# A table-lookup convolution block on one Trainium2 core: the distance matmuls of a step split around the lookup products, and the accumulator given a bank of its own

## The chip, the cores and the metric

The kernel runs on one core of one Trainium2 chip. The time is the device time of one execution in microseconds (us). Before the change it was 2782.4 us, the median of three runs that lie between 2776.88 and 2785.29.

## What is computed

The input x has 16 images of 256 channels and 28x28 pixels. It is normalized over groups of 8 channels (32 groups) and passed through two "convolutions by lookup"; then come a squeeze-and-excite gate and two residual additions. One such convolution, cut to what matters:

```
def amm_conv3x3(x, centroids, w_sub):            # centroids: C x 16 x 9
    p = patches of 3x3, one 9-vector per channel and pixel
    d = |p|^2 - 2 p.centroids + |centroids|^2    # 16 distances per channel, pixel
    attn = softmax(-d)
    lut = einsum('cks,cso->cko', centroids, w_sub)
    return einsum('bnck,cko->bno', attn, lut)
out = relu(bn(amm_conv3x3(gn(x), c1, w1)))
out = bn(amm_conv3x3(out, c2, w2))
out = relu(se(out) + gn(x));  result = x + out
```

The kernel does not build lut. It multiplies the softmax with the centroids again (this gives 9 soft-quantized values per channel and pixel) and then multiplies these by w_sub.

## The kernel before

**Blocks and steps.** An image in a layer is four blocks: two halves of the pixels (392 each, 14 rows) by two halves of the channels (128 each). That is 4 x 16 images x 2 layers = 128 blocks. A block j has two steps, 2j and 2j+1, so there are 256 steps and seven more that only finish the last image. Everything is entered in one table by `at(step, place, function, ...)`; the table is sorted, and each engine issues its instructions in that order, engine by engine, with nothing reordered behind it (`manual_schedule`). So a fractional place such as 0.1 or 2.0 is the order inside one step.

**What TensorE does in a step, in this order.**

- *logits* (places 0.1 and 0.2, line 350 and on, matmul in line 356): two rounds. A round has 16 tiles of 32x32 (4 groups of rows by 4 of columns), each of 392 columns, in 4 PSUM banks. All matmuls are in fp32 and appear as two passes in the profile, so a round is 32 matmul instructions and 32 weight loads, and a step 64 and 64.
- *num_b* (place 1.3, even steps only, line 417): sums of the exponentials, 64 instructions on 64x32 tiles, 2 banks.
- *num_a* (line 403): exponentials by centroids, 64x32 tiles; two calls (32 instructions, 4 banks) in each step.
- *product* (place 2.0, line 485): the lookup product, 9 (or in two steps of each image 3 and 6) full 128x128 matmuls, that is 18 (6, 12) passes, into one bank. An image needs seven such products, because a 2x2 block product is formed with seven multiplications; `mix` (GpSimd, lines 492 and 494) forms the differences of the blocks, and `combine` (line 188) those of the weights S1 to S4 in the first layer.

**The other engines.** ScalarE takes the exponentials out of PSUM (`exps`, line 368, entered right behind each logits round at 0.12 and 0.22), splits num_b's result (lines 428, 430) and copies half of num_a's (line 471). VectorE takes the reciprocal (line 443), spreads it over the rows (lines 454, 458) and scales the other half of num_a's (line 477). GpSimd scales and mixes (lines 466, 492, 494). VectorE or ScalarE take the product out of its bank at place 0.0 of the next step (`acc_add` line 522, `acc_copy` line 516). In the second layer, the first round of half of the blocks is not exponentiated at once: it is copied (`wide_copy`, line 374), its maximum is taken on VectorE, subtracted on GpSimd (line 388) and only then does ScalarE take the exponential (line 396).

**PSUM.** All eight banks form one ring, `bank(name)`; each allocation takes the next bank and waits until what was there eight allocations ago has been read. An even step takes 4 + 4 + 2 + 4 + 1 banks and an odd one 4 + 4 + 4 + 1.

**Loads.** The patches of a step are fetched from DRAM by six transfers (`patches`, lines 342 and 346) from SyncE's queue, issued at place 0.5 two steps ahead, because there are two patch buffers; in the first five steps half of them are issued by GpSimd. SyncE's queue also carries the normalized images (line 335), inputs, stores (line 814) and the preparation of the second layer's tables.

**The end.** For the last image the normalized input is made at place 0.9 of its step 13 (`finish_norm`, line 789), into a buffer that has one copy (`tag="pb"`); flags for the rare unsafe case are made at place 0.95 of its step 11 (`flags`, line 825), into the same buffer. The squeeze-and-excite matmuls (lines 757 and 770) use weights padded to 128 columns.

The lines that set the order of a step's TensorE work:

```
for q in range(2):
    mm = 2 * p + q
    at(g + p, 0.1 + 0.1 * q, logits, u, mm)
    ...
        at(g + p, 0.12 + 0.1 * q, exps, u, mm)
at(g + 2, 1.3, num_b, u)
...
    at(g + 2, 1.35, num_a, u, mm)
...
    at(g + c - (c == 5 and n == 0), 2.0, product, (n, c), us[r], w, ks)
```

Of the kernel before, what the change touches and what calls it, by code (L numbers as in the profile page):

```python
# [23 lines left out]
N = RT * W  # L24
# [12 lines left out]
NPT = 2  # L37
# [30 lines left out]
def kernel(  # L68
# [20 lines left out]
    nc = tc.nc  # L89
    B, C, _ = x.shape  # L90
    NB = C // P
    RED = se_w1.shape[1]

    const = ctx.enter_context(tc.tile_pool(name="const", bufs=1))
    dram = ctx.enter_context(tc.tile_pool(name="dram", bufs=1, space=DRAM))
    small = ctx.enter_context(tc.tile_pool(name="small", bufs=2))
    p_ring = ctx.enter_context(tc.tile_pool(name="p_ring", bufs=8, space=PSUM))

    gmat = const.tile([P, P], F32, name="gmat")
    make_block_diagonal(nc, gmat, 8)  # L100
    ctx.enter_context(tc.manual_schedule())

    def bank(name):
        return p_ring.tile([P, 512], F32, tag="ps", name=name)

    def view(t, off, dims):
# [76 lines left out]
    def combine(n):  # L183
        a, b, op = {
            "S1": ("S3", "A22", ALU.add), "S2": ("S1", "A11", ALU.subtract),
            "S4": ("A12", "S2", ALU.subtract), "S3": ("A11", "S3", ALU.subtract),
        }[n]
        nc.vector.tensor_tensor(wl[n], wl[a], wl[b], op)

    nhalf_sb = load(nhalf, "nhalf_sb")  # L190
    load_wd(None, 0)
# [3 lines left out]
    load_wd(None, 1)  # L195
    load_cw(0, 1)
    vecs = load(vec, "vecs", nc.gpsimd)
    w1_sb = [nhalf_sb, const.tile([P, P], F32, name="w1_sb")]
    w2_sb = const.tile([P, C], F32, name="w2_sb")
    b1_sb = const.tile([P, 1], F32, name="b1_sb")  # L200

    def load_se():
        for t in (*w1_sb, w2_sb, b1_sb):
            nc.gpsimd.memset(t, 0.0)
        for k in range(NB):
            nc.sync.dma_start(w1_sb[k][:, :RED], se_w1[k * P : (k + 1) * P, :])
        nc.sync.dma_start(w2_sb[:RED], se_w2)
        nc.sync.dma_start(b1_sb[:RED], se_b1.rearrange("(p o) -> p o", o=1))


    m_lo, m_hi, zero = kst[:, 0:1], kst[:, 1:2], kst[:, 2:3]
    m_cw = kst[:, 3:7]
# [537 lines left out]

    def se_hidden(b):
        ysum = ys[b, "sum"]
        ps = bank("sep")[:, :1]
        n = 0
        for k in range(NB):
            for i in range(2):
                nc.tensor.matmul(
                    ps, lhsT=w1_sb[k], rhs=ysum[:, k, i : i + 1],
                    start=(n == 0), stop=(n == 2 * NB - 1),
                )  # L760
                n += 1
        hid = small.tile([P, 1], F32, name="se_hid")
        nc.scalar.activation(hid, ps, AF.Relu, bias=b1_sb, scale=1.0 / HW)
        se[b] = hid

    def se_gate(b):
        hid = se[b]
        ps = bank("sep")[:, :NB]
        for k in range(NB):
            nc.tensor.matmul(  # L770
                ps[:, k : k + 1], lhsT=w2_sb[:, k * P : (k + 1) * P], rhs=hid, start=True, stop=True
            )
        gt = small.tile([P, NB], F32, name="se_gt")
        for k in range(NB):
            nc.scalar.activation(
                gt[:, k : k + 1], ps[:, k : k + 1], AF.Exp, bias=nb2_sb[:, k : k + 1], scale=-1.0
            )
        nc.vector.tensor_scalar_add(gt, gt, 1.0)  # L778
        nc.vector.reciprocal(gt, gt)  # L779
        se[b] = gt  # L780
# [4 lines left out]

    def finish_norm(b, k):
        if k == 0:
            ys[b, "t"] = io.tile([P, 1568], F32, tag="pb", name="xn")
        nc.scalar.activation(
            ys[b, "t"][:, HW * k : HW * k + HW], xs[b][:, k], AF.Identity,  # L790
            bias=nrm[:, b, 2, k : k + 1], scale=nrm[:, b, 1, k : k + 1],
        )
# [48 lines left out]
    def at(cl, sub, f, *a, **kw):  # L841
        jobs.setdefault((cl, sub), []).append((f, a, kw))
# [20 lines left out]
    for j, u in enumerate(blocks):  # L863
        g = 2 * j
        u["w"] = j
        wide = u["l"] == 1 and u["hh"] == 0
        for p in range(2):
            u["pt", p] = pts[p]
            at(g + p - NPT, 0.5, patches, u, p, nc.gpsimd if g + p < 5 else None)
            for q in range(2):  # L870
                mm = 2 * p + q
                at(g + p, 0.1 + 0.1 * q, logits, u, mm)
                if wide and mm == 0:
                    at(g, 0.12, wide_copy, u, mm)
# [12 lines left out]
        for mm in range(2):  # L887
            at(g + 2, 1.35, num_a, u, mm)
            at(g + 2, 1.45, copy_a, u, mm)
            at(g + 3, 1.8, spread, u, mm)  # L890
            at(g + 3, 1.8, scale_q, u, mm)
        for mm in range(2, 4):
            at(*((g + 2, 1.8) if mm == 2 else (g + 3, 0.05)), spread, u, mm)
            at(g + 3, 1.0, num_a, u, mm)
            at(g + 3, 1.1, scale_a, u, mm)

    for l in range(2):
        for b in range(B):
# [1 line left out]
            g = 8 * n  # L900
            us = blocks[4 * n : 4 * n + 4]
            for c, (w, r, ks) in PRODUCTS.items():
                at(g + c - (c == 5 and n == 0), 2.0, product, (n, c), us[r], w, ks)
            for mm in (4, 2, 3, 0, 1):
                at(g + 5, 2.5, mix, us[0], mm, us[1], us[0])
                at(g + 7, 2.5 if mm < 2 else 1.75, mix, us[1], mm, us[2], us[1])
# [36 lines left out]
            else:  # L943
# [25 lines left out]
    for hh in range(2):  # L969
        at(6, 2.7, keep_wd, hh)  # L970
    for o in range(2):
# [223 lines left out]
```

## Time and profile before

| | before |
|---|---|
| median of three runs | 2782.4 us |
| the profiled execution's own time | 2758.4 us |
| its span (first to last instruction) | 2756.9 us |
| TensorE busy | 2670.6 us (97%) |
| GpSimd / VectorE / ScalarE busy | 2073.0 / 1730.1 / 1454.2 us (75 / 63 / 53%) |
| DMA engines, mean share in the second half | about 0.5 |
| granted TensorE clock, mean | 0.988 |

The profile shows one execution, which took 2758.4 us, 0.9% less than the median of the runs. "Busy" of TensorE counts time in which some matmul is under way; up to 16 of them are, side by side, and their ends are modelled, so that 97% does not say how full the array is. PEld are TensorE's weight loads. An entry "x64" of the timeline is 64 instructions merged; the first number is the start of the first of them and the second the time to the end of the last. In brackets stands how long the engine sat idle before it and who released it.

### The profile page before, as it was taken

The numbers are of one execution on the slowest core, as the hardware profiler recorded it, in microseconds if no ns is written. First come the engines' busy times: TensorE is split into PE (matmuls) and PEld (weight loads), VectorE is DVE, ScalarE is ACT, GpSimd is POOL, SyncE is SP. The second block draws the span as 40 slices with busy tenths as digits, with TensorE's granted clock in tenths as the row PEclk, the third lists the DMA queues.
The fourth block names the chain that finished last, engine by engine and source line by source line (L and its number), as shares of the span: only waits on it lengthen the run. The fifth ranks groups of instructions, "written<-read, shape, count | busy, mean of one in ns | idle before, by whom it ended". The sixth has DMA issues, their size and how long they took to land. (4 is left out here: it accounts for less than half of the span.)

```text
span 2756.9 us, 88069 instructions
## 1 busy us (share of the span) xinstructions
PE 2670.6 (97%) x37076; PEld 1312.1 (48%) x37076; DVE 1730.1 (63%) x3945; ACT 1454.2 (53%) x3277; POOL 2073.0 (75%) x1427
## 2 busy tenths in 40 slices
PE   5699999999999999999999999999999999999997
PEld 2344444444444444444444455444444444444444
DVE  4866555565655565655576766666766666766664
ACT  3344455545455445455445566656565656555653
POOL 4656877668877767866678787788887788877787
PEclk9899999999999999999999999999999999999998
DMA  8564677546677656666575455445455545555541
GB/s 194 135 131 115 181 196 198 154 110 158 158 189 188 155 125 156 161 165 152 120 182 121 102 120 123 116 103 114 114 120 122 116 105 111 116 118 122 117 106 47
DMA packets 223281, 374.51 MB, mean 136 GB/s; under 512 B 30424, under 2 KB 193592, under 8 KB 222880
## 3 DMA queue, kind: packets, MB, share of 16 engines
q1 hardware_dynamic: 215744, 334.53, 52.6%
q0 software_dynamic: 7136, 34.27, 3.6%
q8 instruction: 296, 4.85, 0.8%
q14 instruction: 105, 0.86, 0.1%
HBM read 288.91 MB, written 79.80 MB: 134 GB/s over the span
## 5 line engine op out<-in xcount | busy, mean ns | idle before, releaser
L368 ACT ACTIVATE e<-lg 128x392 f32<-128x392 f32 x1920 | 777.7, 527 | 814.6 <-PE lg L356 812.3
L494 POOL TENSOR_TENSOR qp<-qp,qp 128x784 f32<-128x784 f32 x512 | 938.6, 1863 | 22.9 <-DVE qp L477 22.9
L485 PE MATMUL acc<-qp,w_S 128*128 128x392 f32 x2048 | 708.3, 496 | 5.2 <-POOL qp L494 5.2
L466 POOL TENSOR_TENSOR qp<-qp,rb 128x784 f32<-128x784 f32 x256 | 470.7, 1861 | 204.4 <-DVE rb L458 204.4
L356 PE MATMUL lg<-pt,wd 32*32 32x392 f32 x16384 | 535.2, 503 | 43.9 <-DVE half_sum L522 18.7
L458 DVE STREAM_SHUFFLE rb<-r 128x392 f32<-128x392 f32 x1024 | 551.2, 603 | 0.0
L485 PEld LDWEIGHTS acc<-qp,w_S 128*128 128x128 f32 x2048 | 387.4, 191 | 306.0 <-issue 15.9
L485 PE MATMUL acc<-qp,w_A 128*128 128x392 f32 x1536 | 521.2, 492 | 0.0
L437 DVE SCALAR_TENSOR_TENSOR r<-nb,kst,r 128x392 f32<-128x392 f32 x128 | 79.8, 623 | 563.4 <-ACT r L428 547.3
L403 PE MATMUL na<-e,cwa 64*32 64x392 f32 x8192 | 409.0, 496 | 3.9 <-issue 3.9
L485 PEld LDWEIGHTS acc<-qp,w_A 128*128 128x128 f32 x1536 | 291.8, 190 | 213.8
L417 PE MATMUL nb<-e,cwb 64*32 64x392 f32 x8192 | 371.2, 496 | 0.0
L356 PEld LDWEIGHTS lg<-pt,wd 32*32 32x32 f32 x16384 | 232.0, 103 | 274.8 <-issue 171.4
L443 DVE RECIPROCAL r<-r 128x392 f32<-128x392 f32 x128 | 331.8, 2592 | 0.0
L466 POOL TENSOR_TENSOR qo<-qo,rb 128x392 f32<-128x392 f32 x128 | 131.1, 1024 | 259.2 <-DVE rb L454 259.1
L477 DVE TENSOR_TENSOR qp<-na,rb 128x392 f32<-128x392 f32 x512 | 252.3, 555 | 64.6 <-PE na L403 61.7
L403 PEld LDWEIGHTS na<-e,cwa 64*32 64x32 f32 x8192 | 146.4, 106 | 230.2 <-ACT e L368 125.0
L417 PEld LDWEIGHTS nb<-e,cwb 64*32 64x32 f32 x8192 | 143.2, 107 | 220.6 <-issue 138.3
L471 ACT COPY qp<-na 128x392 f32<-128x392 f32 x512 | 211.6, 513 | 3.9 <-PE na L403 3.9
L428 ACT ACTIVATE r<-nb,kst 128x392 f32<-128x392 f32 x128 | 87.6, 685 | 102.7 <-PE nb L417 100.1
L492 POOL TENSOR_TENSOR qo<-qo,qo 128x392 f32<-128x392 f32 x128 | 130.8, 1022 | 2.2
L374 ACT COPY e<-lg 128x392 f32<-128x392 f32 x128 | 52.9, 500 | 150.6 <-PE lg L356 150.6
(146 smaller groups left out, 1810.7 us busy)
## 6 DMA issues: line engine op xcount, KB each, us to landing
pt<-home SPq DMA_DIRECT2D x768, 209.0 KB
pt<-home SPq DMA_DIRECT2D x753, 104.5 KB
home<-xpad SPq DMA_DIRECT2D x31, 899.0 KB
xt<-in_x SPq DMA_DIRECT2D x30, 784.0 KB
out_dram<-y SPq DMA_DIRECT2D x32, 392.0 KB
w_S<-d_wS SPq DMA_DIRECT2D x4, 576.0 KB
st<-in_wsub SPq DMA_DIRECT2D x4, 512.0 KB
st<-d_wa SPq DMA_DIRECT2D x16, 128.0 KB
```

The lines of the kernel that those rows point to most:

```text
L356: nc.tensor.matmul(bk[32 * c : 32 * c + 32, :N].rearrange("p (r w) -> p r w", w=W), lhsT=wts["wd", u["hh"]][32 * i : 32 * i + 32, mm, c, : ...
L368: nc.scalar.activation(eg[:, i, :], bk[:, :N], AF.Exp, scale=2.0)
L403: nc.tensor.matmul(bs[r][32 * i : 32 * i + 32, :N], lhsT=wts["cwa", u["hh"]][64 * r : 64 * r + 64, mm, i, :], rhs=es[64 * r : 64 * r + 64, ...
L417: nc.tensor.matmul(bs[r][32 * i : 32 * i + 32, :N], lhsT=wts["cwb", u["hh"]][64 * r : 64 * r + 64, mm, i, :], rhs=es[64 * r : 64 * r + 64, ...
L443: nc.vector.reciprocal(u["r"], u["r"])
L458: nc.vector.stream_shuffle(rb[:, r, :], u["r"], mask_of(2 * mm + r))
L466: nc.gpsimd.tensor_tensor(q, q, u.pop(("rb", mm)), ALU.mult)
L471: nc.scalar.copy(u["q", 2 * mm + r], bk[:, :N])
L477: nc.vector.tensor_mul(u["q", 2 * mm + r], bk[:, :N], rb[:, r, :])
L485: nc.tensor.matmul(accs[key][:, :N], lhsT=wl[w][:, k, :], rhs=us["q", k], start=first and n == 0, stop=last and n == len(ks) - 1,)
L492: nc.gpsimd.tensor_tensor(out_u["q", 8], in0["q", 8], in1["q", 8], ALU.subtract)
L494: nc.gpsimd.tensor_tensor(pair(out_u, mm), pair(in0, mm), pair(in1, mm), ALU.subtract)
```

## The change

1. *Placement.* Each product is issued in two parts (places 2.0 and 2.05, the first with half of the factors, rounded up). The first of a step's two logits rounds moves to place 2.04 of the step before, between these parts; its exponentials follow at 2.06. The second stays at 0.1. So TensorE's order in a step becomes: one logits round, num_b, num_a, first part of the product, the next step's other logits round, second part of the product.
2. *Banks.* The ring has seven banks; the eighth belongs to the product alone.
3. *Combine.* S2 and S4 are formed by GpSimd in place of VectorE; S2 is entered at 2.65 and not 1.96 of step 7.
4. *Squeeze and excite.* The two halves of the weights are stored side by side (32 columns), so that the first product has 32 output rows; the gate takes one matmul in place of two, after one more small ScalarE instruction.
5. *The end.* `finish_norm` of the last image goes to place 0.4 of step 12, `flags` to 0.65 of step 11, and both write into a free buffer of the exponentials in place of the single `pb` buffer.
6. *The start.* The very first step's six patch transfers are all issued from SyncE's queue.

```diff
-    p_ring = ctx.enter_context(tc.tile_pool(name="p_ring", bufs=8, space=PSUM))
+    p_ring = ctx.enter_context(tc.tile_pool(name="p_ring", bufs=7, space=PSUM))
+    p_acc = ctx.enter_context(tc.tile_pool(name="p_acc", bufs=1, space=PSUM))
...
     def bank(name):
+        if name == "acc":
+            return p_acc.tile([P, 512], F32, tag="pa", name=name)
         return p_ring.tile([P, 512], F32, tag="ps", name=name)
...
-        nc.vector.tensor_tensor(wl[n], wl[a], wl[b], op)
+        (nc.gpsimd if n in ("S2", "S4") else nc.vector).tensor_tensor(wl[n], wl[a], wl[b], op)
...
-        ps = bank("sep")[:, :1]
+        ps = bank("sep")[: 2 * RED, :1]
...
-                    ps, lhsT=w1_sb[k], rhs=ysum[:, k, i : i + 1],
+                    ps, lhsT=w1_sb[:, k, :], rhs=ysum[:, k, i : i + 1],
...
-        se[b] = hid
+        se[b] = small.tile([2 * RED, NB], F32, name="se_hh")
+        nc.scalar.activation(se[b], halves, AF.Copy, scale=hid)
...
-        for k in range(NB):
-            nc.tensor.matmul(
-                ps[:, k : k + 1], lhsT=w2_sb[:, k * P : (k + 1) * P], rhs=hid, start=True, stop=True
-            )
+        nc.tensor.matmul(ps, lhsT=w2_sb, rhs=se[b], start=True, stop=True)
...
-            ys[b, "t"] = io.tile([P, 1568], F32, tag="pb", name="xn")
+            if b == B - 1:
+                ys[b, "t"] = epool.tile([P, 4, N], F32, tag="e", name="xn").rearrange("p i n -> p (i n)")
+            else:
+                ys[b, "t"] = io.tile([P, 1568], F32, tag="pb", name="xn")
...
-        ok = io.tile([P, 1568], F32, tag="pb", name="ok")[:, : 16 * B].rearrange("p (a n) -> p a n", a=2)
+        ok = epool.tile([P, 4, N], F32, tag="e", name="ok").rearrange("p i n -> p (i n)")
...
-            at(g + p - NPT, 0.5, patches, u, p, nc.gpsimd if g + p < 5 else None)
+            at(g + p - NPT, 0.5, patches, u, p, nc.gpsimd if 0 < g + p < 5 else None)
             for q in range(2):
                 mm = 2 * p + q
-                at(g + p, 0.1 + 0.1 * q, logits, u, mm)
+                early = (g + p - 1, 2.04)
+                at(*((g + p, 0.1) if q else early), logits, u, mm)
                 if wide and mm == 0:
-                    at(g, 0.12, wide_copy, u, mm)
+                    at(g - 1, 2.06, wide_copy, u, mm)
...
-                    at(g + p, 0.12 + 0.1 * q, exps, u, mm)
+                    at(*((g + p, 0.12) if q else (g + p - 1, 2.06)), exps, u, mm)
...
-                at(g + c - (c == 5 and n == 0), 2.0, product, (n, c), us[r], w, ks)
+                m = (len(ks) + 1) // 2
+                cl = g + c - (c == 5 and n == 0)
+                at(cl, 2.0, product, (n, c), us[r], w, ks[:m], True, False)
+                at(cl, 2.05, product, (n, c), us[r], w, ks[m:], False, True)
...
-                    at(g + (13 if last else 19), 0.9, finish_norm, b, q)
+                    at(*((g + 12, 0.4) if last else (g + 19, 0.9)), finish_norm, b, q)
...
-                    at(g + 11, 0.95, flags)
+                    at(g + 11, 0.65, flags)
...
-    for c, m in ((5, "S1"), (7, "S2"), (8, "S4"), (6, "S3")):
-        at(c, 1.96, combine, m)
+    for c, sub, m in ((5, 1.96, "S1"), (6, 1.96, "S3"), (7, 2.65, "S2"), (8, 1.96, "S4")):
+        at(c, sub, combine, m)
```

More of the change, by code (lines that the diff above doesn't have):

```diff
@@ L197 @@
     vecs = load(vec, "vecs", nc.gpsimd)
-    w1_sb = [nhalf_sb, const.tile([P, P], F32, name="w1_sb")]
-    w2_sb = const.tile([P, C], F32, name="w2_sb")
-    b1_sb = const.tile([P, 1], F32, name="b1_sb")
+    w1_sb = const.tile([P, NB, 2 * RED], F32, name="w1_sb")
+    w2_sb = const.tile([2 * RED, P], F32, name="w2_sb")
+    b1_sb = const.tile([2 * RED, 1], F32, name="b1_sb")
+    halves = const.tile([2 * RED, NB], F32, name="halves")
+    nc.gpsimd.memset(halves, 0.0)
+    nc.gpsimd.memset(halves[:RED, 0:1], 1.0)
+    nc.gpsimd.tensor_scalar(halves[:, 1:2], halves[:, 0:1], -1.0, 1.0, op0=ALU.mult, op1=ALU.add)
     def load_se():
-        for t in (*w1_sb, w2_sb, b1_sb):
-            nc.gpsimd.memset(t, 0.0)
         for k in range(NB):
-            nc.sync.dma_start(w1_sb[k][:, :RED], se_w1[k * P : (k + 1) * P, :])
-        nc.sync.dma_start(w2_sb[:RED], se_w2)
-        nc.sync.dma_start(b1_sb[:RED], se_b1.rearrange("(p o) -> p o", o=1))
+            nc.sync.dma_start(w1_sb[:, :, k * RED : (k + 1) * RED], se_w1.rearrange("(b p) r -> p b r", p=P))
+            nc.sync.dma_start(w2_sb[k * RED : (k + 1) * RED], se_w2[:, k * P : (k + 1) * P])
+            nc.sync.dma_start(b1_sb[k * RED : (k + 1) * RED], se_b1.rearrange("(p o) -> p o", o=1))
     m_lo, m_hi, zero = kst[:, 0:1], kst[:, 1:2], kst[:, 2:3]
@@ L761, in se_hidden @@
                 n += 1
-        hid = small.tile([P, 1], F32, name="se_hid")
+        hid = small.tile([2 * RED, 1], F32, name="se_hid")
         nc.scalar.activation(hid, ps, AF.Relu, bias=b1_sb, scale=1.0 / HW)
-        se[b] = hid
+        se[b] = small.tile([2 * RED, NB], F32, name="se_hh")
+        nc.scalar.activation(se[b], halves, AF.Copy, scale=hid)
     def se_gate(b):
-        hid = se[b]
         ps = bank("sep")[:, :NB]
-        for k in range(NB):
-            nc.tensor.matmul(
-                ps[:, k : k + 1], lhsT=w2_sb[:, k * P : (k + 1) * P], rhs=hid, start=True, stop=True
-            )
+        nc.tensor.matmul(ps, lhsT=w2_sb, rhs=se[b], start=True, stop=True)
         gt = small.tile([P, NB], F32, name="se_gt")
@@ L823, in flags @@
     def flags():
-        ok = io.tile([P, 1568], F32, tag="pb", name="ok")[:, : 16 * B].rearrange("p (a n) -> p a n", a=2)
+        ok = epool.tile([P, 4, N], F32, tag="e", name="ok").rearrange("p i n -> p (i n)")
+        ok = ok[:, : 16 * B].rearrange("p (a n) -> p a n", a=2)
         nc.vector.tensor_scalar(ok[:, 0], wsum, LIM, None, op0=ALU.is_le)
```

## The prediction

> **What bounds the kernel now.** I read the busy shares first, then TensorE's timeline in a quiet stretch, then its idle times, then the start and the end.
>
> ```profile
> PE 2670.6 (97%) x37076; PEld 1312.1 (48%) x37076; DVE 1730.1 (63%) x3945; ACT 1454.2 (53%) x3277; POOL 2073.0 (75%) x1427
> ```
>
> TensorE is the bound. From 601 us to the tail it hardly rests (299.3 of the 300 us from 1000 to 1300, then all), so a gain in the body must come out of how densely its instructions stand. Two steps of the second layer, TensorE's timeline:
>
> ```profile
> 1507.75 2.03 PE L356 MATMUL lg<-pt,wd 32*32 32x392 f32 x64
> 1509.70 2.86 PE L417 MATMUL nb<-e,cwb 64*32 64x392 f32 x64
> 1512.36 1.52 PE L403 MATMUL na<-e,cwa 64*32 64x392 f32 x32
> 1513.81 0.93 PE L485 MATMUL acc<-qo,w_A 128*128 128x392 f32 x2
> 1514.58 5.43 PE L485 MATMUL acc<-qp,w_A 128*128 128x392 f32 x16
> 1519.93 2.02 PE L356 MATMUL lg<-pt,wd 32*32 32x392 f32 x64
> 1521.89 1.64 PE L403 MATMUL na<-e,cwa 64*32 64x392 f32 x32
> ```
>
> From start to start: logits 1.955, num_b 2.66, num_a 1.45 (even) or 1.57 (odd), product 6.12. num_b's 64 instructions are 8 passes of 8 tiles, 0.33 each, so the array is full. The logits' 64 are 4 passes of 16 tiles: at 0.33 they would take 1.31. The weight loads show where 0.64 goes:
>
> ```profile
> 1507.74 0.46 PEld L356 LDWEIGHTS lg<-pt,wd 32*32 32x32 f32 x33 [0.56 <-issue]
> 1508.43 0.63 PEld L356 LDWEIGHTS lg<-pt,wd 32*32 32x32 f32 x31 [0.23 <-issue]
> ```
>
> Round one is loaded in one go; it was queued while the product ran. Of round two one tile is, and the others start, by the trace's single instructions, only at 1508.62, some 17 to 24 ns apart: they enter as round one retires. So a round that is queued in time takes 0.36 (first to second pass) + 0.10 (its 16 starts) + 0.42 (last start to another kind's first) = 0.87, and round two takes 1.27, from 1508.43 to 1509.70.
>
> Two single losses remain, a stall at the start and the tail after the last product:
>
> ```profile
> 93.21 20.26 DVE L188 TENSOR_TENSOR w_S<-w_S,w_A 128x1152 f32<-128x1152 f32 x1
> 114.00 1.53 PE L356 MATMUL lg<-pt,wd 32*32 32x392 f32 x8 [18.67 <-DVE half_sum L522]
> ...
> 2743.01 1.96 ACT L789 ACTIVATE xn<-e,nrm 128x784 f32<-128x784 f32 x2
> 2743.15 1.01 PE L757 MATMUL sep<-ysum,w_sb 128*128 128x1 f32 x4 [1.32 <-ACT y L540]
> ```
>
> The sum below is made against the profiled execution's own 2758.4 us (span 2756.9), which is 0.9% below the median 2782.4; I scale at the end.
>
> **1. Placement.** The gain is round two's wait: both rounds now follow a product part of at least 2 passes and can be queued. The cost is a second break of the product. A product of 18 passes lasts 6.12; one of 12, at 2699.18, ends in 2703.33, so 4.15; hence 0.33 a pass and 0.20 fixed (start and change of tile shape). One more part costs 0.20.
>
> Before: 1.955. After: 2 x 0.87 + 0.20 = 1.94. So the direct gain is 0.01 us a step, 3 us in 255 steps: the price of breaking the product is nearly all of what round two loses.
>
> Here a rule speaks against the change. The Trainium skill (TensorEngine Tiling (Array Packing), section Key Properties) says that changing the tiling mode drains TensorE, and a step has two more changes. It gives no time. TensorE: Matmul & The Clock Gate, section Single matmul latency, puts the part of a warm matmul outside its streaming at about 166 ns; an estimate from it is 2 x 0.17 = 0.33 a step, 85 us. The rows give 0.42 from last start to next first start at a change against 0.33 without, so 0.09 a change, which is inside the 0.87 and 0.20 above. I take the rows: the changes are seen here 3 times a step.
>
> A second-order cost: behind a lone round the next instructions enter as it retires. num_b's 8 tiles, 17 to 24 ns apart as in round two, start over 0.15 and not 0.05, and each tile keeps its delay: +0.10. Even steps: 128 x (0.10 - 0.01) = +11. In odd steps num_a gets the same 0.10, but loses the 0.11 that it now waits (1.57 against 1.45) for round two's exponentials to free banks: 127 x -0.02 = -3. In the second layer even steps mean 1.99 and not 1.955 for the logits, as wide_copy delays what follows; it now runs during the product: about -3. Sum +5; without the smear -20; with twice the smear +30.
>
> **2. Banks.** The product's own bank is a relief: its predecessor must be read before the next product (2.4 us later at least), where now the fourth group of round two waits for it 0.9 us in. Of the ring of seven I counted the reuse. The mid-product round takes, in even steps, the banks of the last logits group, num_b and the first of num_a; by ScalarE's order (four exponentials 1.7, two splits 1.3, copies 0.4 each) these are free some 1.2 us before it in a full product. The round at 0.1 needs in its fourth group what the mid-product round's first exponential frees, 0.93 + 0.53 = 1.5 us after that round's start against 3.6 in a full product. Tight is the step with 3 factors, whose second part has 2 passes: there exponentials, acc_copy and exponentials follow each other on ScalarE and num_a's last bank comes some 0.3 late: 32 x 0.3 = +10, from which I take 8, as part may overlap the smear. Queued behind a waiting tile is all of TensorE. Bounds 0 to +25, the upper for second-layer steps in which wide_exp (1.58), finish_norm (2 x 1.1) and finish_gate (2 x 1.0) stand ahead of the moved exponentials.
>
> **3. Patches.** They are needed some 3 us earlier in relation to their issue, and SyncE's order is unchanged. From the packets' ends, the last one lands some 4 us after the sixth issue; the new use comes a median 8.7 us later, but in ten of 247 steps under 3, in one 1.3 too late. The moved wait would stand in the middle of the product. +2, bounds 0 to +12.
>
> **4. S2 and S4 on GpSimd.** The stall: from 95.4, where num_b would have started, to 115.5 is 20; num_b, at a lower clock, then takes 4.8 in place of 2.7: 22 in all. The Trainium skill (SBUF — State Buffer, section Who interferes with whom) says that a VectorE instruction with two SBUF inputs contends with a GpSimd one that reads SBUF, and that issue order decides who blocks. By the rule alone every combine should be at risk; the rows give 20.26 for S2, 2.32 for S1, 1.42 and 1.77 for the others. S2's 20 us lie beside GpSimd operations without a gap (93.3 to 112.3), so its move helps. On GpSimd the shapes by row (784 elements in 1.86) give 2.7 us each. S2 is then ready after GpSimd's queue, at 115; without the stall the S2 product would be due near 109, so some 5 us of wait return. Behind it stand scale_q and the mixes, which had 13.5 us of idle at 112. Net -17, bounds -22 to -10.
>
> **5. End, start, gate.** flags waits 10.2 us for GpSimd (until 2738.1) and holds VectorE's addition of the next-to-last product to 2739.5, which else could run at 2733.6; then one normalization and the relus are out of the way, and xn no longer stands before se_hid. Se_hid's activation comes some 2.5 us sooner, fewer se instructions save 0.5: -3 (0 to -4). The first patches no longer wait for GpSimd until 20.3: -1 (0 to -2). In the other 15 images the gate matmuls save about what two changes of shape cost: 0.
>
> **Sum.** +5 +8 +2 -17 -3 -1 = -6, so 2752; times 2782.4/2758.4 gives 2776. A time within 0.3% (8.3 us) is about what a measurement here cannot tell from no change. The forecast lies inside, on the faster side.
>
> **Rivals.**
>
> *A: the rounds pay.* No smear, banks in time: placement -20, banks 0, patches 0, -17, -3, -1: -41, so 2717 and 2741. For it: num_b shows no smear today. Against: today its tiles enter before round two ends.
>
> *B, slower: the moved exponentials come late on ScalarE.* A round whose group is not free when the queue reaches it loses round two's 0.40 again. The forecast's margin is 6, so 15 more such rounds turn the sign. If it is all 64 odd second-layer steps and 16 in the first layer: 80 x 0.40 = 32, with the forecast's -6 it gives 2784, hence 2809. For it: ScalarE is at 0.57 to 0.60 in the second layer, and its order now has exponentials twice a step. Against: 2 us of slack in a full product, and ScalarE idles 812 us waiting for logits.
>
> *C: the placement does nothing and only the single losses go.* Placement and banks cancel to 0, patches +2: -19, so 2739, hence 2763.
>
> **How the numbers follow.** Forecast 2768 to 2786: 0.36 (a third of it beyond 0.3% faster). A, and what lies between it and C: 0.15. C: 0.17. B and dearer changes of shape: 0.32. Faster: 0.12 + 0.15 + 0.17 = 0.44; same 0.24; slower 0.32. The range reaches from A's neighbourhood, 2745, to B's, 2812, leaving out a tenth at each end.
>
> **What would show it.** In the timeline: lone rounds of 32 instructions; product parts of 10 and 8 passes, 3.5 and 2.8 from start to start; a round 0.87; num_b 2.76; no L188 on VectorE at 93 and a wait on GpSimd near 109; the tail from the last product 3 us shorter. B would show as lone rounds of 1.2 with loads held by ScalarE. A round of 0.7, or shape changes unlike 0.09, would make the sum wrong; so would GpSimd falling behind after step 7.

## The result and the profile after

The changed kernel takes 2755.6 us (median of four runs, 2752.1 to 2759.3), against 2782.6 for the kernel before (four runs, 2776.9 to 2785.3): a ratio of 0.9906, interval 0.9886 to 0.9926. That is 27 us less, inside the range given, on the faster side, and 20 us below the predicted 2776. Against the profiled execution of before (2758.4) the profiled one of after (2755.55, span 2754.1) is only 2.9 us shorter, where the sum said 6; so most of the 27 us lies in what that one execution of before did not show (see the first experiment).

First the busy shares of the profile after, then TensorE's timeline in the stretch that was shown of before (start, time to the end of the last, engine, line, operation, tile, count):

```profile
PE 2681.2 (97%) x37044; PEld 1283.6 (47%) x37044; DVE 1723.1 (63%) x3943; ACT 1478.2 (54%) x3293; POOL 2074.8 (75%) x1425
```

```profile
1503.33 2.95 PE L421 MATMUL nb<-e,cwb 64*32 64x392 f32 x64
1505.98 1.60 PE L407 MATMUL na<-e,cwa 64*32 64x392 f32 x32
1507.52 0.93 PE L489 MATMUL acc<-qo,w_A 128*128 128x392 f32 x2
1508.28 2.80 PE L489 MATMUL acc<-qp,w_A 128*128 128x392 f32 x8
1511.01 0.94 PE L360 MATMUL lg<-pt,wd 32*32 32x392 f32 x32
1511.88 2.90 PE L489 MATMUL acc<-qp,w_A 128*128 128x392 f32 x8
1514.71 0.94 PE L360 MATMUL lg<-pt,wd 32*32 32x392 f32 x32
```

From start to start: num_b 2.65, num_a 1.54 (1.45 before), product parts 3.49 and 2.83, a lone round 0.87. The share of TensorE is 97% as before, although the kernel is faster: overlapped instructions are counted once, so the share does not show density.

The stall at the start is gone. This is TensorE's timeline there, with S2 among the combined weights behind it (durations in ns, first and last start):

```profile
109.14 2.90 PE L489 MATMUL acc<-qp,w_S 128*128 128x392 f32 x8
...
116.03 0.93 PE L489 MATMUL acc<-qo,w_S 128*128 128x392 f32 x2 [1.55 <-POOL w_S L191]
```

```profile
L191 POOL TENSOR_TENSOR w_S<-w_S,w_A x1: 2625/2625/2625, 113.4 to 113.4; 128x1152 f32<-128x1152 f32 x1
```

S2 takes 2.63 us on GpSimd, where it took 20.26 on VectorE, and what returns as a wait for it is 1.55, not 5.

Something new appears once in each image of the second layer. All engines there, by the timeline:

```profile
1993.44 1.51 ACT L400 ACTIVATE e<-e 128x1568 f32<-128x1568 f32 x1 [0.96 <-DVE e L396]
...
1994.86 1.96 ACT L793 ACTIVATE xn<-xt,nrm 128x784 f32<-128x784 f32 x2
...
1996.72 1.77 ACT L785 ACTIVATE y<-y,se_gt 128x784 f32<-128x784 f32 x2
...
1999.51 1.68 PE L360 MATMUL lg<-pt,wd 32*32 32x392 f32 x32
1999.79 3.15 ACT L372 ACTIVATE e<-lg 128x392 f32<-128x392 f32 x8
2000.32 0.15 PEld L360 LDWEIGHTS lg<-pt,wd 32*32 32x32 f32 x8 [0.61 <-ACT e L372]
2001.11 2.86 PE L421 MATMUL nb<-e,cwb 64*32 64x392 f32 x64
```

ScalarE works through the wide exponential (line 400), the last normalization (line 793) and the gate (line 785) before it comes to the exponentials of the round in the middle of the product. So at 1999.51 the other round finds a bank still unread, its last loads wait for line 372, and num_b starts 1.60 after the round, not 0.87. That is rival B's mechanism, in one round of an image.

### The profile page after: what moved, and what is told of

It is laid out like the page before. It is cut to its first block, busy times and chain, and to the rows that moved or that the text cites. A ratio compares the mean times of both kernels' runs of the same rounds, so it can differ in the third digit from the quotient of the medians.

```text
span 2754.1 us, 87843 instructions
## 1 busy us (share of the span) xinstructions
PE 2681.2 (97%) x37044; PEld 1283.6 (47%) x37044; DVE 1723.1 (63%) x3943; ACT 1478.2 (54%) x3293; POOL 2074.8 (75%) x1425
## 4 chain that ended last, share of the span: by engine, by line
PE 89%; POOL 4%; DMA 3%; DVE 1%; SPq 1%; issue 1%; ACT 0%; POOLq 0%; ACTq 0%
PE acc L489 48%; PE lg L360 16%; PE nb L421 13%; PE na L407 12%; DMA pt<-home 2%; POOL qp L498 2%; POOL qp L470 1%; DMA home<-hpad,col 1%; SPq L346 1%; DMA home<-xpad 1%; DVE st L712 0%; SPq L350 0%; POOL qo L496 0%; DVE rb L462 0%; PE sep L761 0%
## 5 line engine op out<-in xcount | busy, mean ns | idle before, releaser
L372 ACT ACTIVATE e<-lg 128x392 f32<-128x392 f32 x1920 | 798.8, 506 | 916.9 <-PE lg L360 916.5
L489 PE MATMUL acc<-qp,w_S 128*128 128x392 f32 x2048 | 752.6, 506 | 2.2 <-POOL qp L498 2.1
L489 PE MATMUL acc<-qp,w_A 128*128 128x392 f32 x1536 | 546.4, 499 | 0.0
L360 PE MATMUL lg<-pt,wd 32*32 32x392 f32 x16384 | 504.5, 506 | 30.7 <-DMA pt<-home 23.5
L407 PE MATMUL na<-e,cwa 64*32 64x392 f32 x8192 | 422.0, 494 | 1.7 <-ACT e L372 0.9
L421 PE MATMUL nb<-e,cwb 64*32 64x392 f32 x8192 | 384.5, 498 | 1.7 <-issue 1.6
L421 PEld LDWEIGHTS nb<-e,cwb 64*32 64x32 f32 x8192 | 205.6, 107 | 171.5 <-issue 83.8
L407 PEld LDWEIGHTS na<-e,cwa 64*32 64x32 f32 x8192 | 199.1, 106 | 179.1 <-issue 88.2
L360 PEld LDWEIGHTS lg<-pt,wd 32*32 32x32 f32 x16384 | 126.0, 103 | 299.4 <-issue 247.3
L526 DVE TENSOR_TENSOR y<-acc,y 128x392 f32<-128x392 f32 x80 | 43.8, 564 | 153.1 <-PE acc L489 111.2
```

The costliest lines, as they stand in the source:

```text
L360: nc.tensor.matmul(bk[32 * c : 32 * c + 32, :N].rearrange("p (r w) -> p r w", w=W), lhsT=wts["wd", u["hh"]][32 * i : 32 * i + 32, mm, c, : ...
L372: nc.scalar.activation(eg[:, i, :], bk[:, :N], AF.Exp, scale=2.0)
L407: nc.tensor.matmul(bs[r][32 * i : 32 * i + 32, :N], lhsT=wts["cwa", u["hh"]][64 * r : 64 * r + 64, mm, i, :], rhs=es[64 * r : 64 * r + 64, ...
L421: nc.tensor.matmul(bs[r][32 * i : 32 * i + 32, :N], lhsT=wts["cwb", u["hh"]][64 * r : 64 * r + 64, mm, i, :], rhs=es[64 * r : 64 * r + 64, ...
L489: nc.tensor.matmul(accs[key][:, :N], lhsT=wl[w][:, k, :], rhs=us["q", k], start=first and n == 0, stop=last and n == len(ks) - 1,)
```

## The experiments

Differences of medians are taken against the kernel before, run alternately on the same chip. Its medians there are 2776.7 (first set, from "before, again" to "rounds side by side"), 2777.0 (second set, to "ring of eight") and 2765.5 (third set, the rest), and 2782.6 beside the changed kernel. The chips differ, so times of different sets are not compared, ratios are. The four right-hand columns are worked out from one trace each: where the num_b of block 8, of block 64 (the second layer's first) and of the last block start, and the span's end, less the same of the first profile of before, so that each column is what one stretch gained or lost.

| kernel | median, us | minus before | ratio (interval) | to block 8 | 8 to 64 | layer 2 | tail |
|---|---|---|---|---|---|---|---|
| before, again | 2776.4 | -0.4 | 0.9998 (0.9988–1.0008) | -4.0 | +15.6 | +0.8 | 0.0 |
| changed | 2755.6 | -27.0 | 0.9906 (0.9886–0.9926) | -22.7 | +15.5 | +5.1 | -0.8 |
| before + combine | 2762.3 | -14.4 | 0.9943 (0.9927–0.9960) | -19.7 | +14.6 | +0.8 | 0.0 |
| before + placement and banks | 2788.0 | +11.3 | 1.0036 (1.0024–1.0049) | -11.8 | +21.2 | +12.7 | +7.4 |
| changed, rounds side by side | 2812.3 | +35.5 | 1.0125 (1.0104–1.0145) | -20.4 | +40.1 | +36.6 | -0.8 |
| small edits only | 2754.8 | -22.1 | 0.9924 (0.9911–0.9938) | -14.8 | +21.5 | -5.0 | -3.7 |
| changed, late normalization | 2747.4 | -29.6 | 0.9891 (0.9872–0.9910) | -23.9 | +12.9 | +0.5 | -0.5 |
| small edits, scatter later | 2766.8 | -10.1 | 0.9965 (0.9952–0.9979) | -14.2 | +31.7 | -3.3 | -3.7 |
| changed, ring of eight | 2750.1 | -26.9 | 0.9904 (0.9889–0.9919) | -20.7 | +14.7 | +3.8 | -4.2 |
| changed, ring of eight and late | 2736.8 | -28.7 | 0.9904 (0.9884–0.9923) | -29.0 | +8.0 | -4.0 | -4.0 |
| before + squeeze-and-excite | 2758.5 | -7.0 | 0.9975 (0.9958–0.9992) | -1.4 | +6.1 | -5.0 | 0.0 |
| small edits, late | 2737.8 | -27.7 | 0.9902 (0.9881–0.9924) | -13.0 | +11.4 | -5.4 | -3.7 |
| placement in layer 1 only, ring of eight | 2735.2 | -30.3 | 0.9897 (0.9877–0.9916) | -24.6 | +14.4 | -5.8 | -3.6 |

The columns of the second layer and the tail repeat to about 1 us between kernels that are alike there; those of the first layer do not, and no conclusion rests on less than 5 us in them.

**The kernel before, once more** (nothing edited).

> The kernel before, unchanged. Its profiled execution took 2758.4 us and its timed ones 2777 to 2785; the changed kernel's profile (2755.6) and times (2752 to 2759) agree. Theory S (the start): the VectorE combine that stalled TensorE for 18.7 us in the profile stalls it longer in other executions; then a new profile near 2780 shows one longer stall before 130 us and the body unchanged. Theory P (the body): a profile near 2780 shows the steps themselves longer, by some 0.09 us each. Theory N (chance): the first profile was an unusual execution by its granted clock; then a profile near 2780 shows a lower clock and everything stretched.

Measured: 2776.4, ratio 0.9998. Its profiled execution took 2770.85, and its trace is 15.6 us longer than the first profile between blocks 8 and 64. The loss comes in pieces of 0.4 to 1.9 us, at the logits rounds beside which GpSimd issues a scatter (an indirect DMA). TensorE, its loads and GpSimd at one of them:

```profile
962.96 3.32 PE L356 MATMUL lg<-pt,wd 32*32 32x392 f32 x64
963.65 0.46 PEld L356 LDWEIGHTS lg<-pt,wd 32*32 32x32 f32 x16 [0.23 <-issue]
...
964.03 1.03 POOL L548 DMA_INDIRECT home<-hpad,col  x1 [0.16 <-PE lg L356]
...
964.58 0.15 PEld L356 LDWEIGHTS lg<-pt,wd 32*32 32x32 f32 x4 [0.48 <-issue]
965.32 0.24 PEld L356 LDWEIGHTS lg<-pt,wd 32*32 32x32 f32 x11 [0.59 <-issue]
```

Round two's loads stop twice, by 0.48 and 0.59, for "issue", that is for nothing that the profile shows, while GpSimd issues the scatter of line 548. The two rounds take 3.25 from start to start and not 1.96. In the first profile the step with the same scatter loses nothing (1.95 from start to start):

```profile
956.03 2.03 PE L356 MATMUL lg<-pt,wd 32*32 32x392 f32 x64
956.31 1.03 POOL L548 DMA_INDIRECT home<-hpad,col  x1
```

Over all such steps between blocks 8 and 64 (those beside a stretch of lower granted clock left out), the 20 with a scatter take 19.6 us more than the median step in this trace, and 19 take 1.2 more in the first profile; the 90 and 92 without one take 4.0 and 7.0 more. So the profile that I summed against was an execution nearly free of these losses. The granted clock (mean 0.990 here, 0.988 there) does not explain the difference.

**Combine alone.**

```diff
-        nc.vector.tensor_tensor(wl[n], wl[a], wl[b], op)
+        (nc.gpsimd if n in ("S2", "S4") else nc.vector).tensor_tensor(wl[n], wl[a], wl[b], op)
...
-    for c, m in ((5, "S1"), (7, "S2"), (8, "S4"), (6, "S3")):
-        at(c, 1.96, combine, m)
+    for c, sub, m in ((5, 1.96, "S1"), (6, 1.96, "S3"), (7, 2.65, "S2"), (8, 1.96, "S4")):
+        at(c, sub, combine, m)
```

> Before with the combine edit alone (S2 and S4 on GpSimd, S2 at place 2.65). By the prediction's sum -17 us. Theory S: the whole of the 24 us between profile and times of before goes with it, so -35 to -45, about 2742. Theory P: -15 to -20 alone, about 2765. Theory N: -15 to -20, with the same spread of times as before.

Measured: -14.4, all of it before block 8 (-19.7 against -4.0 of the unedited kernel in that set, so -15.7 by the traces). The term is confirmed, some 2 us under its size. Of the 15.7, 11.5 are idle time of TensorE; the rest is about what the half clock around the end of the stall costs (granted clock 0.50 from 97.5 to 117.5 us in the trace of the unedited kernel).

**Placement and banks alone** (the diff of the change, parts 1 and 2, on the kernel before).

> Before with the placement alone: product in two parts, one logits round between them, ring of seven and a bank for the product; no other edit. By the prediction's sum +15 us (2797). By the two profiles, in which the changed kernel gives back some 18 us after its early lead, +15 to +18. Theory P: it takes the 24 us of the body away, so -10 to -5 (2775). Theory S: +15 (2797).

Measured: +11.3, slower by itself, and near the +15 of the prediction's sum. By the traces it has +11.9 in the second layer and +7.4 in the tail against the unedited kernel of the same set, and -7.8 and +5.6 in the two stretches of the first. In the tail the product's own bank is no relief: the last product waits for it until VectorE, held up by `flags`, has added the product before.

```profile
2761.46 0.56 DVE L525 TENSOR_TENSOR y<-acc,y 128x392 f32<-128x392 f32 x1
2762.17 1.64 PE L488 MATMUL acc<-qo,w_A 128*128 128x392 f32 x2 [4.60 <-DVE y L525]
```

In the changed kernel, where `flags` comes earlier, no wait of this length is left.

**The changed kernel without the placement** (both rounds at 0.1 and 0.2 again, the product in one part; ring of seven and the product's own bank kept).

```diff
-                early = (g + p - 1, 2.04)
-                at(*((g + p, 0.1) if q else early), logits, u, mm)
+                at(g + p, 0.1 + 0.1 * q, logits, u, mm)
...
-                    at(*((g + p, 0.12) if q else (g + p - 1, 2.06)), exps, u, mm)
+                    at(g + p, 0.12 + 0.1 * q, exps, u, mm)
```

> The changed kernel with the placement undone (both logits rounds at the head of the step, product in one part), ring of seven, product's own bank and the four small edits kept. By the prediction's sum -21 us to before: 2761. By the profiles' lead before the body gives it back, -20 to -25. Theory S: 2738 or below, faster than the changed kernel. Theory P: 2760, slower than the changed kernel.

Missed by far: 35.5 above before. Its loads in a step of the second layer show the reason:

```profile
2008.62 0.46 PEld L360 LDWEIGHTS lg<-pt,wd 32*32 32x32 f32 x33 [0.56 <-issue]
2009.31 0.54 PEld L360 LDWEIGHTS lg<-pt,wd 32*32 32x32 f32 x23 [0.23 <-issue]
2010.16 0.15 PEld L360 LDWEIGHTS lg<-pt,wd 32*32 32x32 f32 x8 [0.32 <-ACT e L372]
2010.95 0.18 PEld L407 LDWEIGHTS na<-e,cwa 64*32 64x32 f32 x16 [0.64 <-ACT e L372]
```

With seven banks the last group of round two needs the bank that round one's first exponential frees. The logits take a mean of 2.29 in 112 steps of the second layer against 1.96: 112 x 0.33 = 37 us in 14 images. So ring and placement belong together, and this run says nothing on the placement by itself; the next does.

**The small edits alone** (the changed kernel less parts 1 and 2; ring of eight).

> The changed kernel without the placement and with the ring of eight again: the four small edits alone. The run with combine alone gave -14 to -16 us against before; the squeeze-and-excite rows of the two traces give -0.5 us an image, -8; the end -3. Theory 'the small edits carry the gain': 2747 to 2752, a little faster than the changed kernel. Rival 'the placement carries it': 2760 or more. It also prices the ring: the same kernel with seven banks and a bank for the product took 2812, so if this gives 2750, the ring of seven costs 60 us, 0.24 a step, where both rounds stand side by side (the fourth group of round two then takes the bank of round one's first).

Measured: 0.9924, where the changed kernel has 0.9906, with overlapping intervals: the small edits carry the gain, and placement with banks adds nothing that can be told. In the traces they cancel by stretch: placement with banks has -7.9 before block 8, -6.0 to block 64, +10.1 in the second layer and +2.9 in the tail.

**Late normalization.**

```diff
-                    at(*((g + 12, 0.4) if last else (g + 19, 0.9)), finish_norm, b, q)
+                    at(*((g + 12, 0.4) if last else (g + 19, 2.2)), finish_norm, b, q)
                     if not last:
-                        at(g + 19, 0.91, finish_gate, b, q)
+                        at(g + 19, 2.21, finish_gate, b, q)
```

> The changed kernel, with finish_norm and finish_gate of the second layer entered behind the moved exponentials (2.2 in place of 0.9 of step 19). In the changed kernel's trace one round in each second-layer image waits 0.74 us, with ScalarE busy on wide_exp, these four and two normalizations ahead of its exponentials. Theory 'late exponentials': that wait goes, 15 x 0.74 = -11 against the changed kernel, 2745. Rival (the wait has another cause, or a new one follows behind the relu that waits on GpSimd): 2755.

Measured: 0.9891, which the medians cannot tell from the changed kernel. By the trace, the stall before num_b is gone (all 56 rounds before num_b in 14 images take 0.87), which is worth 9.5 us there; 3.3 come back, as one half of the product with six factors now takes 2.29 and not 2.17 in the mean. In the second layer 4.6 are left.

**The scatter later.** The scatter of step 13 goes from place 2.4 to 2.9, in the kernel of the small edits.

> The small edits alone, and one of the four scatters of the first layer's result on GpSimd's queue moved behind the mixes (2.9 in place of 2.4 of step 13). In before's second profile, and not in its first, round two lost 1.25 us once an image in the first layer while that scatter was issued beside it. Theory 'the scatter disturbs the round': these losses go, about -15 to the run with the small edits alone, near 2735. Rival (they only coincide, the cause is elsewhere): 2750, the losses stay.

Missed: 12 us slower than the small edits. The pauses stay, each beside a scatter (18.9 us in 15 steps, where the small edits have 22.6 in 21), and TensorE's idle time between blocks 8 and 64 grows from 12.0 to 19.9 us, as products now wait for GpSimd's mixes:

```profile
906.83 3.63 PE L486 MATMUL acc<-qp,w_S 128*128 128x392 f32 x5 [5.30 <-POOL qp L495]
```

Only one scatter of four was moved, so the run shows that this place is no remedy, and leaves open whether the scatters set off the pauses.

**Ring of eight.** The product goes back into the common ring, the placement stays.

> The changed kernel with the product in the ring of eight again, placement kept. The fourth group of the round behind the product then takes the product's bank and must wait until VectorE or ScalarE has read it, some 0.7 us into the round. Theory 'the own bank is what lets the lone round pay': +0.5 to +0.8 a step, +130 to +200, near 2900. Rival (the reads come in time): 2755 or less, since the ring is longer.

Missed by 150 us: 0.9904, like the changed kernel, with 1.3 us less in the second layer and 3.4 less in the tail. My picture of the ring does not hold for this kernel: in the second layer, the last group of the round behind the product waits for ScalarE in all 122 steps between 1440 and 2700 us, also in the 90 in which VectorE reads the product. So the product's bank is not the next in turn there. (In the kernel before that group does wait for the engine that reads the product, in all 122 steps, as the section on that kernel says; how the banks are given out no run shows.) The product needs no bank of its own.

**Ring of eight and late normalization together.**

> The changed kernel with two edits together: the product back in a ring of eight banks, and the last normalization of the second layer's images (finish_norm, finish_gate) entered behind the moved exponentials. Alone they gave -5.5 (2750.1) and -8.2 us (2747.4) against the changed kernel's 2755.6. Theory 'they are two different waits' (the first gives more slack on banks everywhere, the second ends the one late exponential per second-layer image): 2742, faster than all kernels so far. Rival 'both work on the same late round': 2747, no better than the second alone. In the trace both theories want every logits round of the second layer at 0.87 from start to start.

By the medians no better than each alone (0.9904). By the trace the second layer has 9.1 us less than the changed kernel, where the two alone have 4.6 and 1.3: with eight banks the returned wait is 0.6 in 14 images and not 3.3. This is a timeline at the place of the stall, ScalarE and TensorE:

```profile
1979.37 1.67 ACT L369 ACTIVATE e<-lg 128x392 f32<-128x392 f32 x4 [0.39 <-PE lg L357]
1980.90 1.99 ACT L790 ACTIVATE xn<-xt,nrm 128x784 f32<-128x784 f32 x2
1982.14 0.94 PE L357 MATMUL lg<-pt,wd 32*32 32x392 f32 x32
...
1983.02 2.95 PE L418 MATMUL nb<-e,cwb 64*32 64x392 f32 x64
```

The exponentials now stand before the normalization, and num_b starts 0.88 after the round.

**Squeeze and excite alone** (part 4 on the kernel before).

> The kernel before with the squeeze-and-excite edit alone (weights side by side, 32 output rows, one gate matmul). The trace of the changed kernel has these matmuls' stretch 0.5 us shorter in each image, against the 0 that was forecast: theory 'this is real and on TensorE's path': 16 x 0.5 = 8 less than before, 2768 to 2769 where before has 2776.7. Rival 'the time goes into the next step, as logits then wait longer for something else' (the forecast's 0): 2776.

Measured: -7.0 (ratio 0.9975, interval -11.6 to -2.2 us), with -5.0 in the second layer by the trace. TensorE's timeline in before and in the changed kernel:

```profile
1694.62 0.50 PE L757 MATMUL sep<-ysum,nhalf_sb 128*128 128x1 f32 x4
1694.98 0.58 PE L757 MATMUL sep<-ysum,w_sb 128*128 128x1 f32 x4
1695.49 2.02 PE L356 MATMUL lg<-pt,wd 32*32 32x392 f32 x64
```

```profile
1690.23 0.41 PE L761 MATMUL sep<-ysum,w_sb 128*32 128x1 f32 x8
1690.57 0.94 PE L360 MATMUL lg<-pt,wd 32*32 32x392 f32 x32
```

Eight matmul instructions with 128 output rows hold the logits for 0.87 us, eight with 32 rows for 0.34. With the gate (0.43 and 0.31), less 0.19 by which the products before them grow, an image gains 0.47; 0.12 of it return in num_a, and 0.35 an image are left in the small edits (0.30 in this run), 5 to 6 us in all.

**Small edits and late normalization.**

> The four small edits without placement and bank change (2754.8), with finish_norm and finish_gate of the second layer entered late as in the kernel that gained 8 us. Theory 'the late exponential hurts only a round that stands alone in the product': no gain, 2753 to 2757. Rival 'finish_norm at that place costs in any order of the rounds': some 8 less, 2747.

The trace sides with the first theory: -5.4 in the second layer against -5.0 without it. The medians leave it open (0.9902 against 0.9924, intervals overlap). The trace also shows something else. In the first layer the program is that of the small edits, but the scatters cost next to nothing: 2.3 us in 21 steps, against 22.6. Here is the same pair of rounds in the small edits and in this run; in both a scatter (line 629) starts 0.17 after the rounds:

```profile
327.55 3.94 PE L357 MATMUL lg<-pt,wd 32*32 32x392 f32 x64
327.72 1.01 POOL L629 DMA_INDIRECT d_sk<-st,col  x1 [0.15 <-issue]
```

```profile
330.82 2.14 PE L357 MATMUL lg<-pt,wd 32*32 32x392 f32 x64
330.99 1.01 POOL L629 DMA_INDIRECT d_sk<-st,col  x1
```

Squeeze and excite alone, from the same chip, shows the same (1.9 us in 19 steps). So a scatter beside the rounds does not cost in every execution.

**Placement in the first layer only.**

```diff
-                early = (g + p - 1, 2.04)
-                at(*((g + p, 0.1) if q else early), logits, u, mm)
+                early = q == 0 and u["l"] == 0
+                at(*((g + p - 1, 2.04) if early else (g + p, 0.1 + 0.1 * q)), logits, u, mm)
```

> The changed kernel with the product in the ring of eight, and the moved logits round in the first layer only; in the second layer both rounds stand side by side as before. Theory 'the placement gains only what the first layer loses where rounds stand side by side, and costs in the second': the first layer as in the changed kernel, the second shorter by 0.4 to 0.9 us an image, so 7 to 14 less than the 2750.1 of the ring of eight with both layers moved: 2736 to 2743. Rival 'placement costs nothing in the second layer once the banks are free': 2750; and if the losses of the first layer return in the second: above 2755.

The second layer comes out as forecast, -5.8 against +3.8; the total, 0.9897, cannot be told from the 0.9904 of the ring of eight, where 7 to 14 us were expected. In this set, on one chip, three kernels with the same small edits stand side by side: rounds moved everywhere 2736.8, nowhere 2737.8, in the first layer only 2735.2 (the first two with late normalization). Where the rounds stand makes no difference that can be measured there, once the waits of the moved rounds are taken away; on this chip, though, the traces show next to none of the pauses that the placement could save. No version was shown to beat the changed kernel: the best ratios, 0.9891 and 0.9897, overlap with 0.9906.

## Why the prediction was right, and where not

The direction was right, and the range held. The case that came is nearest to rival C: placement and banks close to nothing beside the small edits, and the gain from these (-22.1 alone, -27 in all; C said -19). That the sum's +15 for placement, banks and patches came to nothing there is in part luck: gains and losses that it did not contain nearly cancel.

*The scaling failed most.* "Times 2782.4/2758.4" added 24 us, as if each part of an execution were slower by the same share. The traces put it elsewhere: in the first layer, where the second profile of before is 15.6 us longer, through pauses of round two that the first profile mostly lacked. The changed kernel's profiled execution lies at its median (2755.55 and 2755.6). Against the second profile of before (2770.85) it is 15.3 shorter, against the medians 27. I should have taken the profile's early finish as a sign of losses that vary, and asked where they can lie.

*Placement, the direct part: right.* A round 0.87, parts of 10 and 8 passes 3.49 + 2.83 = 6.32 against 6.12, so 0.20 for the break. Two rounds and a break are 1.94, as forecast.

*First layer: two things that the sum lacked.* A lone round beside a scatter loses nothing (0.0 in 7 of them, in the changed kernel and with placement alone), and the 34 calls of num_a that now stand beside one lose 3.7 in all, so the placement saves most of the pauses. But TensorE's idle time between blocks 8 and 64 grows, from 12.0 us with the small edits alone to 20.7 in the changed kernel, and behind the longer waits the granted clock is half (0.50 from 284 to 290.5 us in the changed kernel):

```profile
285.24 1.72 PE L360 MATMUL lg<-pt,wd 32*32 32x392 f32 x32 [3.85 <-DMA pt<-home]
286.88 4.75 PE L489 MATMUL acc<-qp,w_S 128*128 128x392 f32 x8
```

These eight passes take 4.68 to the next start and not 2.83. An estimate of the loss is half of the time in which matmuls run at the clock of 0.5: 8.4 against 4.9 us. So against the small edits the stretch has +8.8 of idle time, +3.5 of clock and, as the remainder, -18.3: together -6.0. On the kernel before it is +12.4, +6.3 and -13.1: together +5.6.

*Smear: the mechanism right, the place wrong, the size about half.* num_b stays at 2.66, where 2.76 was forecast. num_a behind it takes 1.536 in place of 1.453 in the median. Over the 112 steps of 14 images num_a is 1.9 us longer than with the small edits alone; I had taken +11 - 3 for 255 steps, which is 3.5 for 112.

*Second layer.* The working had logits at 1.99 in even steps there, and a gain of 3. In the trace of before the even steps take a mean of 1.964. There was next to nothing to win.

*Banks: near in size by luck, wrong in the step.* +8 was put on the product with three factors, for which the runs show no wait (its second part 0.86, next matmul on time). The cost comes from the wait that I had kept for the upper bound, the normalization and the gate ahead of the moved exponentials: 0.68 in each of 14 images, 9.5 us. Rival B was thus right about the mechanism, and wrong about its reach: 14 rounds, not 80. The sum of the second layer closes: against the small edits, over 112 steps, the rounds gain 24.4, lose 9.5 to late exponentials, the breaks cost 22.1 and num_a 1.9: +9.1, and from the num_b of block 68 to that of block 124 the two traces differ by 9.1 (1160.7 and 1151.6).

*The product's own bank as "a relief": wrong*, by the run with the ring of eight and by the last product's wait with placement alone.

*Patches: inside the bounds, but in one stretch more than was said.* The groups of the logits, idle time at the end with its releasers, in the small edits alone and in the changed kernel:

```profile
L357 PE MATMUL lg<-pt,wd 32*32 32x392 f32 x16384 | 557.6, 503 | 24.4 <-DMA pt<-home 20.0 <-DVE hpad L523 2.3 <-DMA st<-d_wa 1.9
```

```profile
L360 PE MATMUL lg<-pt,wd 32*32 32x392 f32 x16384 | 504.5, 506 | 30.7 <-DMA pt<-home 23.5 <-DMA st<-d_wa 4.3 <-DVE qo L444 2.5
```

3.5 us more wait for patches with the placement; +2 was said, up to +12. Between blocks 8 and 64 alone it is 6.3 more (8.1 against 1.8, and 10.4 against 1.0 on the kernel before), and the half clock behind these waits was in no term. The row also shows what the placement does to the eye: busy time of the logits falls by 53 us, and the time of the kernel does not.

*Combine: right* (-17 forecast, -14.4 measured). The rule that was weighed there (the Trainium skill, SBUF — State Buffer, section Who interferes with whom) names the contention; the row of 20.26 set the sum. That contention made S2 slow was not tested apart; the run shows that the stall goes when S2 leaves VectorE.

*Gate matmuls: mis-sized.* "What two changes of shape cost: 0" measured 0.35 an image by the traces, 7.0 in all by the medians. I had looked at the changes of shape only; what shrank with the matmuls is their weight loads, from 0.19 each (128 columns) to 0.11 (32).

*End: right by itself.* The tail has -3.7 in the small edits (-3 forecast). In the changed kernel 2.9 of it are lost again; with the ring of eight they are not (-4.2), so it is the banks and not the placement that lengthen the tail: with the product's own bank three products of the tail wait before they start, by 1.13, 0.72 and 0.75, and with the ring of eight none does. The chain there, from the last gate matmuls on:

```profile
2741.97 0.29 PE L761 MATMUL sep<-ysum,w_sb 128*32 128x1 f32 x4 [1.42 <-ACT y L544]
...
2743.34 0.41 ACT L776 ACTIVATE se_gt<-sep,nb_sb 128x1 f32<-128x1 f32 x2 [0.47 <-PE sep L773]
```

From the first of these matmuls to the gate it is 1.37, where it was 3.07, since ScalarE is free when they end.

*Start: nothing that can be told.* In the changed kernel the first logits begin at 26.2 us and not at 28.9, but the first num_b at 42.5, where it was 42.8.

*On the rule of the tiling mode* (the Trainium skill, TensorEngine Tiling (Array Packing), section Key Properties): the sum of the second layer closes with the 0.09 us a change that the rows gave, inside the 0.87 and the 0.20. At the 0.17 that I had estimated from the other page, 255 steps with two more changes would have cost 85 us, and no run of the placement shows that.

**What stays open.** Why round two's loads pause beside a scatter in four traces with rounds side by side and eight banks (from two chips), and hardly in three others (two from a third chip, and the first profile of before). Each kernel left a single trace, so whether the chip or the execution decides was not shown. How much of the pauses' saving the medians would show without the waits of the placement was not run on the chips that have them.

## What to carry to other kernels

A profile that is faster than every timed run is a warning: compare a second execution before scaling a sum by its ratio to the median, and ask which stretch varies. When a small piece of work is put in the middle of a longer run of matmuls, subtract the price of the break (here 0.20 us, of the 0.21 by which a pair of rounds at 1.955 is longer than two lone ones at 0.87), and then look at what stands in the reader engine's queue ahead of it; with the breaks, that set the second layer's loss. Count with a wait of TensorE also the lower clock behind it. And the small edits, which took single waits and slow loads off the path, were worth all of what could be measured.

## What was not expected of the hardware

- VectorE's S2 took 20.26 us beside a dense run of GpSimd operations; the same 128x1152 subtraction takes 2.63 us on GpSimd.
- The delay of a late start behind a lone round of 16 small tiles does not show in the next 64 instructions as a whole (2.66 as before), but in the group after them (+0.08).
- The logits' loads stop by 0.48 and 0.59 us with nothing in the profile to wait for, beside GpSimd's issue of a scatter: 18 to 23 us between blocks 8 and 64 in four traces, 1 to 2 us in three others with the same scatters.
- Behind a wait of 3.85 us TensorE's granted clock was 0.50 for the next 6 us, and eight passes took 4.68 us where they take 2.83.
- Eight instructions of one-column fp32 matmuls hold the engine for 0.87 us with 128 output rows and 0.34 with 32.
